# A four-layer hybrid of scans, convolutions and an FFT on one core: all stages rewritten with channels on partitions, norms by matrix products, and another packing of the scan

## The chip, the cores and the metric

The kernel runs on one core of one Trainium2 chip, in one launch. The metric is the device time in microseconds (us) of one execution. Everything is computed in fp32 except the two feed-forward blocks, which the reference quantizes (fp8 products, fp16 sums).

## The reference

The input `x` has 4 batches of 96 channels on a 64 x 64 grid, so 4096 positions a batch. Four layers follow each other:

```
# layer 0: state-space block in four directions, then a Gelu mlp
t = layernorm(x); xi, z = split(in_proj(t))            # 192 channels each
xi = silu(depthwise_conv3x3(xi))
for k in 4 directions:                                  # rows, columns, both reversed
    dts, Bs, Cs = x_proj[k](xi)                         # 6 + 16 + 16 rows
    dt = softplus(dt_proj[k](dts))                      # 192 channels
    h  = scan over 4096 positions:  h*exp(dt*A) + dt*B*x    # 192 channels x 16 states
    y += sum over states of h*C,  + D*x
t = x + out_proj(layernorm(y) * silu(z));  x = t + mlp(layernorm(t))   # 96 -> 384 -> 96
# layer 1: x + scan block in two directions with one state, conv 3x3, group norm before, layer norm + gate after
# layer 2: t + attention by FFT: relu(bn(x w1)), fft over 4096 positions, relu of a complex
#          scaling, inverse fft, w2, bn;   then t + quantized ffn(norm(t))
# layer 3: t + linear attention with 6 heads (q (k^T v)), then t + quantized ffn(norm(t))
```

The scan of layer 0 is the bulk: 4 batches x 4 directions x 192 channels x 16 states, each 4096 positions long.

## The kernel before

For each batch the stages run one after another: `l0_front`, `l0_scan`, `l0_tail`, `l1`, `l2_front`. Then one `l2_middle` handles the 64 middle frequencies of all four batches, and for each batch `l2_back`, `ffn`, `l3_attn`, `ffn` and `finish` end the work. A tile framework puts the waits; each engine takes its instructions in the order in which the code emits them. On SP the transfers are issued in that order too.

**Norms.** Layer norms reduce over channels, so `to_tokens` transposes 128 positions at a time through TensorE (L134), `normalize` makes the statistics with bn_stats (L148) and scales token by token on VectorE (L154), and `to_channels` transposes back (L162).

**Front.** The depthwise convolution is nine matmuls with diagonal weights (`dg`, made on GpSimd) for each block of 512 positions, accumulated in PSUM (L220). It runs for three groups of 64 channels, contracting 64 rows, and writes each result to 128 partitions, twice the same 64 channels: the scan wants them doubled.

**Scan.** Partitions are (2 states, 64 channels). A step takes 1024 positions of one direction; there are 4 directions x 4 steps a batch. The prelude of a step computes `px` (L266, with strided reads of `xi` in the column directions), copies it to `xd` on ScalarE (L271), sends B and C to DRAM, computes `dt` (L284 to L289) and `u` (L291). Then come 8 pairs of states x 3 channel groups = 24 iterations:

```
act(h, dts[d], AF.Exp, scale=negA[...])       # ScalarE, into PSUM (2 buffers)
nc.gpsimd.tensor_mul(w, us[d], bb)            # L310
nc.vector.tensor_tensor_scan(h, h, w, ...)    # L315 reversed, L319 forward
nc.scalar.copy(state, last column of h)       # L322, not in a direction's last step
nc.vector.tensor_mul(w, h, cc)                # L323
```

`bb` and `cc` are rows of B and C, spread over 64 partitions by DMA from DRAM. The sum over states is a matmul with a stacked identity (`idup`, L329 and L334) that accumulates in PSUM over the whole step; at the end of a step VectorE adds the sums to `y01` and `y2` (L337, L340).

**The rest.** `l0_tail` computes the gate z from the norm it kept in DRAM (`xn_d`), gates, projects and runs the mlp. `l1` works on whole rows of 4096 positions: its convolution is L465, its output projection L528. The FFT is split as 64 x 64: `l2_front` does the first half, `l2_middle` the twiddled second half and the inverse's first half, `l2_back` the inverse's second half (L656). `ffn` rounds to fp16 and fp8 on ScalarE and VectorE (L702 to L711).

Of the kernel before, what the change touches and what calls it, by code (L numbers as in the profile page):

```python
# [10 lines left out]
F32 = mybir.dt.float32  # L11
F16 = mybir.dt.float16
# [8 lines left out]
NB = L // 128  # L21
DI = 192
NS = 16
CH = 1024
NCH = L // CH
WBUFS = 6
POOL_OUT = 0
TABLES = {AF.Exp: "natural_log_exp_and_others", AF.Ln: "natural_log_exp_and_others"}
OTHER = (AF.Silu, AF.Gelu, AF.Sqrt)

_VECS = [
    ("g1", 1), ("b1", 1), ("bi01", 1), ("bi2", 1), ("bz01", 1), ("bz2", 1),
    ("cw01", 9), ("cw2", 9), ("cb", 3), ("dtb", 12), ("A", 96), ("D01", 4), ("D2", 4),
    ("og01", 1), ("ob01", 1), ("og2", 1), ("ob2", 1), ("opb", 1), ("g2", 1), ("b2", 1),
    ("mb1", 3), ("mb2", 1),
    ("l1cw", 9), ("l1cb", 1), ("l1dtb", 2), ("l1A", 2), ("l1D", 2), ("l1og", 1), ("l1ob", 1),
    ("l1sc", 1), ("f2b1", 3), ("f3b1", 3),
# [9 lines left out]
def tile_hybrid(ctx: ExitStack, tc: tile.TileContext, I: dict, out: bass.AP):  # L49
    nc = tc.nc  # L50
    n_evac = [0]

    def evac(o, i):
        n_evac[0] += 1
        if n_evac[0] % 2:
            nc.scalar.copy(o, i)
        else:
            nc.vector.tensor_copy(o, i)

    table = dict(now=None, load=None, users=[])  # L60
# [23 lines left out]
    const = ctx.enter_context(tc.tile_pool(name="const", bufs=1))  # L84
    dram = ctx.enter_context(tc.tile_pool(name="dram", bufs=1, space=DRAM))

    ident = const.tile([128, 128], F32, name="ident")
    make_identity(nc, ident)

    idup = const.tile([128, 2, 64], F32, name="idup")  # L90
    for h in range(2):
        s = slice(h * 64, h * 64 + 64)
        for j in range(2):
            nc.vector.tensor_copy(idup[s, j, :], ident[s, s])
    eps5 = const.tile([128, 1], F32, name="eps5")
    nc.vector.memset(eps5, 1e-5)
    one = const.tile([128, 1], F32, name="one")
    nc.vector.memset(one, 1.0)
    vec = const.tile([128, NVEC], F32, name="vec")
    nc.sync.dma_start(vec, I["vec"])  # L100

    def V(name, rows=128, j=0, n=1):
        c, w = _COL[name]
        assert j + n <= w
        return vec[0:rows, c + j : c + j + n]

    xn_d = dram.tile([B, C, L], F32, name="xn_d")
    t_d = dram.tile([B, 128, NB * C], F32, name="t_d")
    f1_d = dram.tile([64, 2, 64, B, DI], F32, name="f1_d")
    g1_d = dram.tile([B, 2, 64, 64, DI], F32, name="g1_d")  # L110


    negA = const.tile([128, 96], F32, name="negA")
    act(negA, V("A", n=96), AF.Exp)
    nc.vector.tensor_scalar_mul(negA, negA, -1.0)
    l1A = const.tile([128, 2], F32, name="l1A")
    act(l1A, V("l1A", n=2), AF.Exp)
    nc.vector.tensor_scalar_mul(l1A, l1A, -1.0)
    dsum = const.tile([128, 3], F32, name="dsum")
    nc.vector.reduce_sum(dsum[:, 0:1], V("D01", n=4), axis=mybir.AxisListType.X)  # L120
    nc.vector.reduce_sum(dsum[0:64, 1:2], V("D2", 64, n=4), axis=mybir.AxisListType.X)
    nc.vector.reduce_sum(dsum[0:C, 2:3], V("l1D", C, n=2), axis=mybir.AxisListType.X)


    def to_tokens(srcs, width, xt, ps):

        per = 4 if width == C else 2
        for g in range(NB // per):
            pt = ps.tile([128, 512], F32, tag="ps", name="pt_in")
            for j in range(per):  # L130
                blk = g * per + j
                off = j * width
                for ap, rows in srcs:
                    nc.tensor.transpose(  # L134
                        pt[:, off : off + rows], ap[:, blk * 128 : blk * 128 + 128], ident[:rows, :rows]
                    )
                    off += rows
            evac(
                xt[:, g * per : (g + 1) * per, :],
                pt[:, 0 : per * width].rearrange("p (j c) -> p j c", c=width),  # L140
            )

    def normalize(xt, xn, pool):
        stats = pool.tile([128, NB, 6], F32, tag="lnst", name="lnst")
        mv = pool.tile([128, NB, 2], F32, tag="lnmv", name="lnmv")
        rs = pool.tile([128, NB], F32, tag="lnrs", name="lnrs")
        for k in range(NB):
            nc.vector.bn_stats(stats[:, k, :], xt[:, k, :])  # L148
        for k in range(NB):
            nc.vector.bn_aggr(mv[:, k, :], stats[:, k, :])  # L150
        act(rs, mv[:, :, 1], AF.Sqrt, bias=eps5)
        nc.vector.reciprocal(rs, rs)
        for k in range(NB):
            nc.vector.tensor_scalar(  # L154
                xn[:, k, :], xt[:, k, :], mv[:, k, 0:1], rs[:, k : k + 1], ALU.subtract, ALU.mult
            )

    def to_channels(xn, g, off, rows, ps):

        pt = ps.tile([128, 512], F32, tag="ps", name="pt_out")  # L160
        for j in range(4):
            nc.tensor.transpose(pt[0:rows, j * 128 : j * 128 + 128], xn[:, 4 * g + j, off : off + rows], ident)  # L162
        return pt[0:rows, :]

# [7 lines left out]

    def psum(name, bufs):
        return dict(name=name, bufs=bufs, space=PSUM)

    def l0_front(b, xi):
        st, (wp, wk, ps) = pools(sb("l0f"), sb("l0f2", 2), psum("l0fp", 8))  # L180
        w_in = wp.tile([C, DI], F32, name="w_in")
        nc.sync.dma_start(w_in, I["w_inT"][:, 0:DI])
        x = wp.tile([C, L], F32, name="x")
        for q in range(4):
            nc.sync.dma_start(x[:, q * CH : (q + 1) * CH], I["x"][b, :, q * CH : (q + 1) * CH])
        xt = wp.tile([128, NB, C], F32, name="xt")
        to_tokens([(x, C)], C, xt, ps)
        normalize(xt, xt, wp)

        dg01 = wp.tile([128, 9, 128], F32, name="dg01")  # L190
        dg2 = wp.tile([64, 9, 128], F32, name="dg2")
        idf = idup.rearrange("p a b -> p (a b)")
        for t in range(9):
            nc.gpsimd.tensor_scalar(dg01[:, t, :], idf, V("cw01", 128, t), None, ALU.mult)  # L194
            nc.gpsimd.tensor_scalar(dg2[:, t, :], idf[0:64], V("cw2", 64, t), None, ALU.mult)
        xp01 = wp.tile([128, 66, 66], F32, name="xp01")
        xp2 = wp.tile([64, 66, 66], F32, name="xp2")
        nc.gpsimd.memset(xp01, 0.0)
        nc.gpsimd.memset(xp2, 0.0)
        for g in range(8):  # L200
            pt = to_channels(xt, g, 0, C, ps)
            xn = wk.tile([C, 512], F32, tag="xn", name="xn")
            act(xn, pt, AF.Identity, scale=V("g1", C), bias=V("b1", C))
            nc.sync.dma_start(xn_d[b, :, g * 512 : (g + 1) * 512], xn)
            for xp, m0, m, bias in ((xp01, 0, 128, V("bi01")), (xp2, 128, 64, V("bi2", 64))):
                pi = ps.tile([128, 512], F32, tag="ps", name="pi")
                nc.tensor.matmul(pi[0:m], lhsT=w_in[:, m0 : m0 + m], rhs=xn, start=True, stop=True)
                nc.vector.tensor_scalar(
                    xp[:, 1 + 8 * g : 9 + 8 * g, 1:65],
                    pi[0:m].rearrange("p (h w) -> p h w", w=64), bias, None, ALU.add,  # L210
                )

        for d in range(3):
            r0 = 64 if d == 1 else 0
            xp, dg = (xp2, dg2) if d == 2 else (xp01, dg01)
            for g in range(8):
                pc = ps.tile([128, 512], F32, tag="ps", name="pc")
                for t in range(9):
                    kh, kw = divmod(t, 3)
                    nc.tensor.matmul(  # L220
                        pc.rearrange("p (h w) -> p h w", w=64),
                        lhsT=dg[r0 : r0 + 64, t, :],
                        rhs=xp[r0 : r0 + 64, 8 * g + kh : 8 * g + kh + 8, kw : kw + 64],
                        start=(t == 0), stop=(t == 8),
                    )
                act(xi[d][:, g * 512 : (g + 1) * 512], pc, AF.Silu, bias=V("cb", 128, d))
        st.close()

    def l0_scan(b, xi, y01, y2):


        st, (ck, wk, ph, ps, dp) = pools(
            sb("l0c", 2), sb("l0w", WBUFS), psum("l0hp", 2), psum("l0sp", 1),
            dict(name="l0d", bufs=3, space=DRAM),
        )
# [5 lines left out]
        for k in range(4):  # L241
# [7 lines left out]
            def view(ap, lo, n):  # L249

                if not col:
                    return ap[:, lo : lo + n]
# [669 lines left out]
```

## Time and profile before

| | |
|---|---|
| median of 3 runs | 11,112.8 us (11,093.09 to 11,119.98) |
| profiled execution | 11,114.38 us, span 11,112.6 us |
| mean granted TensorE clock | 0.692 of full |
| VectorE (DVE) busy | 7171.7 us, 65% |
| TensorE (PE) busy | 8037.6 us, 72% |
| GpSimd (POOL) busy | 4701.3 us, 42% |
| ScalarE (ACT) busy | 3760.3 us, 34% |
| DMA | 713.27 MB, mean 64 GB/s |

The profile is one execution. Its slices cut the span into 40 equal parts, each digit the busy tenths of an engine; PEclk is the granted TensorE clock in tenths. A group row gives line, engine, operation, output and inputs, count, busy time, the mean duration in ns of one, and the idle time of the engine just before with what ended it. A row of windows gives, for a stretch of the span, its length, each engine's busy time, the granted clock, the share of the DMA engines and GB/s. Each fp32 matmul shows as two records. The batches follow each other about 2413 us apart; the middle of layer 2 begins at 9677 us and the four backs at 9993 us.

### The profile page before, as it was taken

What the parts mean: (1) busy time and instruction counts of PE and PEld (TensorE: products, weight loads), DVE (VectorE), ACT (ScalarE), POOL (GpSimd) and SP (SyncE); (2) the same over time, 40 slices, a digit from 0 to 9 for tenths busy, and PEclk for the clock granted to TensorE, in tenths of its full rate; (3) what the DMA queues carried; (4) which work ended last, traced back from release to release, by engine and by line L of the source; (5) the groups of instructions that cost most, each with busy time, mean ns of one, the idle gap of its engine ahead of it and who ended that gap; (6) DMA issues with size and microseconds to landing.
All of it is one profiled execution on the core that took longest, in us unless ns stands there. A gap on an engine that the chain in (4) does not pass through costs nothing. (4 is left out here: it accounts for less than half of the span.)

```text
span 11112.6 us, 64945 instructions
## 1 busy us (share of the span) xinstructions
PE 8037.6 (72%) x18840; PEld 2774.3 (25%) x18840; DVE 7171.7 (65%) x8167; ACT 3760.3 (34%) x5408; POOL 4701.3 (42%) x2174
## 2 busy tenths in 40 slices
PE   9776675869776766788766767697766768696666
PEld 3111111233111112233111112242111112244445
DVE  1688888340888887322888895415888883425555
ACT  1444443221444442213444442214444432211111
POOL 0677775000777772003777771005777750020000
PEclk9666666867667667757666667667666668695555
DMA  0233332010333331011333330012333330261110
GB/s 12 74 90 86 89 88 76 4 42 9 93 87 89 89 89 51 1 42 40 89 87 89 88 90 25 14 29 65 87 88 89 89 85 5 55 189 48 38 37 30
DMA packets 270938, 713.27 MB, mean 64 GB/s; under 512 B 49638, under 2 KB 106480, under 8 KB 269172
## 3 DMA queue, kind: packets, MB, share of 16 engines
q1 hardware_dynamic: 262388, 683.95, 23.1%
q0 software_dynamic: 8192, 25.17, 0.6%
q8 instruction: 149, 2.44, 0.1%
q14 instruction: 209, 1.71, 0.1%
HBM read 631.34 MB, written 77.59 MB: 64 GB/s over the span
## 5 line engine op out<-in xcount | busy, mean ns | idle before, releaser
L310 POOL TENSOR_TENSOR w<-u,bb 128x1024 f32<-128x1024 f32 x1536 | 3574.7, 2350 | 1323.7 <-PE py L329 1133.9
L329 PE MATMUL py<-w,idup 128*64 128x512 f32 x4096 | 2374.7, 965 | 1165.1 <-DVE w L323 1157.1
L75 ACT ACTIVATE h<-dt,negA 128x1024 f32<-128x1024 f32 x1536 | 1703.5, 1117 | 954.5 <-DVE w L323 947.3
L323 DVE TENSOR_TENSOR w<-h,cc 128x1024 f32<-128x1024 f32 x1536 | 1800.6, 1210 | 217.4 <-ACT state L322 217.4
L334 PE MATMUL py<-w,idup 128*64 128x512 f32 x2048 | 1144.1, 909 | 586.8 <-DVE w L323 586.8
L319 DVE TENSOR_TENSOR_SCAN h<-h,state,w 128x1024 f32<-128x1024 f32 x576 | 1324.3, 2345 | 97.8 <-ACT h L75 69.2
L315 DVE TENSOR_TENSOR_SCAN h<-h,state,w 128x1024 f32<-128x1024 f32 x576 | 1324.4, 2345 | 77.2 <-ACT h L75 50.0
L329 PEld LDWEIGHTS py<-w,idup 128*64 128x64 f32 x4096 | 524.3, 192 | 2858.7 <-DVE w L323 1796.7
L319 DVE TENSOR_TENSOR_SCAN h<-h,w 128x1024 f32<-128x1024 f32 x192 | 431.9, 2287 | 1211.9 <-POOL w L310 1152.6
L289 POOL TENSOR_TENSOR dt<-dt,rl 128x1024 f32<-128x1024 f32 x192 | 451.3, 2350 | 1796.5 <-DMA cc<-bc 790.4
L220 PE MATMUL pc<-xp,dg 64*128 64x512 f32 x1728 | 975.6, 750 | 0.0
L266 PE MATMUL px<-xi,xw 64*80 64x512 f32 x768 | 685.6, 1010 | 61.9 <-ACT state L322 29.5
L284 PE MATMUL pd<-xd,dtw 6*128 6x512 f32 x768 | 561.4, 818 | 183.9 <-ACT rl L67 142.9
L322 ACT COPY state<-h 128x1 f32<-128x1 f32 x1152 | 183.1, 159 | 1467.3 <-DVE h L315 768.7
L220 PEld LDWEIGHTS pc<-xp,dg 64*128 64x128 f32 x1728 | 403.6, 237 | 575.1 <-issue 574.0
L334 PEld LDWEIGHTS py<-w,idup 128*64 128x64 f32 x2048 | 250.6, 187 | 1186.5 <-DVE w L323 852.5
L291 POOL TENSOR_TENSOR u<-dt,xi 128x1024 f32<-128x1024 f32 x192 | 499.1, 2599 | 11.0
L67 ACT ACTIVATE dt<-pd,vec 128x512 f32<-128x512 f32 (+1 forms) x448 | 307.5, 686 | 531.8 <-PE pd L284 320.9
L315 DVE TENSOR_TENSOR_SCAN h<-h,w 128x1024 f32<-128x1024 f32 x192 | 430.0, 2285 | 44.5 <-ACT h L75 36.7
L194 POOL TENSOR_SCALAR dg<-idup,vec 128x128 f32<-128x128 f32 x36 | 21.4, 596 | 847.4 <-issue 847.0
L75 ACT ACTIVATE xi<-pc,vec 128x512 f32<-128x512 f32 x96 | 66.0, 687 | 893.2 <-PE pc L220 893.2
L621 POOL DMA_DIRECT2D g_d<-o x128 | 79.3, 624 | 603.4 <-DVE o L619 597.4
(210 smaller groups left out, 8339.2 us busy)
## 6 DMA issues: line engine op xcount, KB each, us to landing
bb<-bc SPq DMA_DIRECT2D x1024, 256.0 KB
cc<-bc SPq DMA_DIRECT2D x1024, 256.0 KB
f_d<-fo SPq DMA_DIRECT2D x64, 384.0 KB
a<-f_d SPq DMA_DIRECT2D x64, 384.0 KB
g_d<-o POOLq DMA_DIRECT2D x128, 192.0 KB, 4.0
gt<-g_d SPq DMA_DIRECT2D x32, 768.0 KB
bc<-xd SPq DMA_DIRECT2D x128, 64.0 KB
x<-in_x SPq DMA_DIRECT2D x16, 384.0 KB
```

Of the source, the lines that this page charges most:

```text
L75: r = nc.scalar.activation(o, i, func, **kw)
L220: nc.tensor.matmul(pc.rearrange("p (h w) -> p h w", w=64), lhsT=dg[r0 : r0 + 64, t, :], rhs=xp[r0 : r0 + 64, 8 * g + kh : 8 * g + kh + 8, ...
L266: nc.tensor.matmul(like(px[0:80]), lhsT=xw[:, d, :], rhs=view(xi[d][0:64], lo + hf * 512, 512), start=(d == 0), stop=(d == 2),)
L284: nc.tensor.matmul(pd, lhsT=dtw[:, d, :], rhs=xd[0:6, s], start=True, stop=True)
L289: nc.gpsimd.tensor_add(dt, dt, rl)
L291: nc.gpsimd.tensor_mul(like(u), like(dt), view(xi[d], lo, CH))
L310: nc.gpsimd.tensor_mul(w, us[d], bb)
L315: nc.vector.tensor_tensor_scan(o[:, ::-1], h[:, ::-1], w[:, ::-1], first, ALU.mult, ALU.add)
L319: nc.vector.tensor_tensor_scan(o, h, w, first, ALU.mult, ALU.add)
L323: (nc.gpsimd if pool_out else nc.vector).tensor_mul(w, o, cc)
L329: nc.tensor.matmul(py01[d * 64 : d * 64 + 64, s], lhsT=idup[:, 0, :], rhs=ws[d][:, s], **flags)
L334: nc.tensor.matmul(py2[hf * 64 : hf * 64 + 64], lhsT=idup[:, 0, :], rhs=ws[2][:, s], **flags)
```

## The change

The kernel is rewritten. Positions stay on the free axis and channels on partitions in all stages, so `to_tokens`, `normalize` and `to_channels` go. The main pieces:

- **Norm.** A matmul with the centring matrix `cent`, a Square on ScalarE, a matmul with `avg` for the variance, Ln and Exp(-0.5 x) on ScalarE, a multiply on VectorE.
- **Front.** Convolution of 128 channels at a time, then 64 channels x 2 halves of the grid. The gate z is computed here and kept in DRAM (`z_d`). `xi` goes to DRAM in row order and in column order (`xi_d`); GpSimd makes the transposed copy.
- **Scan.** Partitions are (32 channels, 4 states). Two times 3 groups of 32 channels x 4 quartets of states = 24 iterations a step as before, but `dt`, `u`, `bb` and `cc` are all spread by DMA from DRAM, the prelude works on [128, 3, 512] without doubling, the state copy is issued behind the C product, and the reduction is two matmuls of 32 columns an iteration with `sel4` that end after four iterations. The Y addition runs three times a step, into `Y` in SBUF. The prelude of the next step is emitted piece by piece between the iterations (`advance`). Y goes to DRAM at the end (`y_d`).
- **Tail, l1, FFT, back.** Each block of 512 positions goes through its whole chain before the next; `x1_d`, `t_d` and `t2_d` in DRAM hold the blocks between stages. `l2_middle` runs for each batch, so its tables `wf` and `wi` are loaded four times. The stages are generators; `drain` runs one to its end before the next begins (`OVERLAP` is False).

The core of the diff:

```diff
-    def to_tokens(srcs, width, xt, ps): ...
-    def normalize(xt, xn, pool): ...
-    def to_channels(xn, g, off, rows, ps): ...
+    def norm(x, o, wk, **kw):
+        pc = bank()
+        mm(pc[0:C], lhsT=cent, rhs=x, start=True, stop=True)
+        yield
+        sq = wt(wk, C, "sq")                      # (inside variance)
+        act(sq, pc[0:C], AF.Square)
+        pv = bank()
+        mm(pv[0:C], lhsT=avg, rhs=sq, start=True, stop=True)
+        yield
+        act(rs, pv[0:rows], AF.Ln, bias=eps5[0:rows])     # (inside rstd)
+        act(rs, rs, AF.Exp, scale=-0.5)
+        nc.vector.tensor_tensor(o, pc[0:C], rs, ALU.mult, **kw)
...
     # front, convolution
-        for d in range(3):
-            r0 = 64 if d == 1 else 0
-            xp, dg = (xp2, dg2) if d == 2 else (xp01, dg01)
-            for g in range(8):
-                for t in range(9):
-                        lhsT=dg[r0 : r0 + 64, t, :],
-                        rhs=xp[r0 : r0 + 64, 8 * g + kh : 8 * g + kh + 8, kw : kw + 64],
+        for part in range(2):
+            rows = 64 if part == 0 else 32
+            xp = (xp01, xp2)[part]
+            for g in range(0, rows // 8, 2):
+                for i in range(2):
+                    for t in range(9):
+                            lhsT=dg[:, t, :],
+                            rhs=xp[:, r : r + 8, kw : kw + 64],
...
     # scan, one iteration
-                        act(h, dts[d], AF.Exp, scale=negA[:, k * 24 + j : k * 24 + j + 1])
-                        nc.gpsimd.tensor_mul(w, us[d], bb)
-                            nc.vector.tensor_tensor_scan(o, h, w, first, ALU.mult, ALU.add)
-                            nc.scalar.copy(state[:, j : j + 1], o[:, last : last + 1])
-                        (nc.gpsimd if pool_out else nc.vector).tensor_mul(w, o, cc)
+                    act(h, dt, AF.Exp, scale=negA[:, k * 24 + n : k * 24 + n + 1])
+                    nc.gpsimd.tensor_mul(w, u, d["bb", q])
+                        nc.vector.tensor_tensor_scan(h, h, w, first, ALU.mult, ALU.add)
+                    nc.vector.tensor_mul(w, h, d["cc", q])
+                    if s < NCH - 1:
+                        nc.scalar.copy(state[:, n : n + 1], h[:, last : last + 1])
+                    for f in range(2):
+                        r = p * 64 + f * 32
+                        if col:
+                            o = py[r : r + 32].rearrange("p (w c h) -> p w c h", c=4, h=8)
+                            v = w.rearrange("p (w c f h) -> p f w c h", c=4, f=2, h=8)[:, f]
+                        else:
+                            o, v = py[r : r + 32], w[:, f * HC : (f + 1) * HC]
+                        mm(o, lhsT=sel4, rhs=v, start=(q == 0), stop=(q == 3))
+                    if n >= 3:
+                        advance(i + 1)
...
     # scan, prelude of a step
+            px = bank()
+            for j in range(3):
+                mm(px, lhsT=xw[:, j, :], rhs=xi[:, j, :], start=(j == 0), stop=(j == 2))
+            act(xd, px, AF.Identity, bias=V("ones"))
+            for j in range(3):
+                mm(pd, lhsT=dtw[:, j, :], rhs=xd[0:64], start=True, stop=True)
+                act(dtu[:, 0, j], pd, AF.Abs)
+                act(rl[:, j], pd, AF.Relu)
+            act(dtu[:, 0], dtu[:, 0], AF.Exp, scale=-1.0)
+            act(dtu[:, 0], dtu[:, 0], AF.Ln, bias=one)
+            nc.gpsimd.tensor_add(dtu[:, 0], dtu[:, 0], rl)
+            nc.gpsimd.tensor_mul(dtu[:, 1], dtu[:, 0], xi)
...
+        def load_du(i, m):                        # one group of four iterations ahead
+                nc.sync.dma_start(x, src.unsqueeze(1).to_broadcast([32, 4, CH]))
...
     # order of the stages
-    l2_middle()
+    for b in range(B):
+        n1 = drain(front(b), 8)
+        scan(b, sp, lambda: None)
+        n2 = drain(post(b), 8)                    # tail, l1, l2_front, l2_middle, back
```

In `back`, the first loop takes each block of 512 through projection, `ffn` of layer 2 (with its norm), the norm of layer 3 and the sum of k^T v; the second loop takes it through the attention's output and the `ffn` of layer 3 (with its norm).

## The prediction

> **What bounds the kernel now.** I read the page's busy totals and slices first, then the stage windows, then the groups of instructions.
>
> ```profile
> PE 8037.6 (72%) x18840; PEld 2774.3 (25%) x18840; DVE 7171.7 (65%) x8167; ACT 3760.3 (34%) x5408; POOL 4701.3 (42%) x2174
> PE   9776675869776766788766767697766768696666
> DVE  1688888340888887322888895415888883425555
> ```
>
> No engine bounds the whole. Four plateaus with DVE at 0.8 are the four scans; the valleys between them, and the last 1,100 us, belong to no engine. So each stage needs its own sum. The windows of batch 0, then the middle of all batches and the back of batch 0:
>
> ```profile
> core 0: us, PE busy (x) PEld busy (x) DVE busy (x) ACT busy (x) POOL busy (x), PEclk, DMA share, GB/s
> 63.00:310.00 247.00, 247.00 (x436) 101.04 (x436) 1.50 (x2) 24.28 (x26) 0.00 (x0) 1.00 0.00 1
> 337.00:1892.00 1555.00, 1062.20 (x1902) 245.32 (x1902) 1367.55 (x816) 691.46 (x983) 1126.22 (x479) 0.67 0.33 88
> 1990.00:2049.00 59.00, 50.71 (x128) 21.37 (x128) 13.54 (x41) 23.96 (x33) 0.00 (x0) 0.93 0.00 0
> 9677.00:9993.00 316.00, 304.02 (x768) 126.30 (x768) 61.31 (x64) 52.42 (x65) 78.36 (x127) 0.97 0.65 188
> 10057.00:10086.00 29.00, 25.53 (x120) 25.28 (x119) 7.31 (x26) 0.00 (x0) 0.00 (x0) 0.50 0.04 13
> 10086.00:10158.00 72.00, 34.04 (x180) 18.39 (x180) 61.22 (x255) 18.97 (x37) 0.00 (x0) 0.53 0.01 3
> ```
>
> The depthwise convolution (first row) is pure PE at full clock; the scan (second) has DVE busy 88%; where PE is busy half of a stage (last row) the granted clock is 0.53, where it is busy 0.86 to 0.96 it is 0.93 to 0.97, though the short matmuls of the row from 10057 stayed at 0.50 with PE busy 88%.
>
> ```profile
> L323 DVE TENSOR_TENSOR w<-h,cc 128x1024 f32<-128x1024 f32 x1536 | 1800.6, 1210 | 217.4 <-ACT state L322 217.4
> L319 DVE TENSOR_TENSOR_SCAN h<-h,state,w 128x1024 f32<-128x1024 f32 x576 | 1324.3, 2345 | 97.8 <-ACT h L75 69.2
> L310 POOL TENSOR_TENSOR w<-u,bb 128x1024 f32<-128x1024 f32 x1536 | 3574.7, 2350 | 1323.7 <-PE py L329 1133.9
> L75 ACT ACTIVATE h<-dt,negA 128x1024 f32<-128x1024 f32 x1536 | 1703.5, 1117 | 954.5 <-DVE w L323 947.3
> L220 PE MATMUL pc<-xp,dg 64*128 64x512 f32 x1728 | 975.6, 750 | 0.0
> L465 PE MATMUL pc<-xp,dg 96*96 96x512 f32 x576 | 247.9, 592 | 0.0
> L528 PE MATMUL po<-yn,w_out 96*96 96x512 f32 x64 | 64.5, 1111 | 72.4 <-DVE yn L526 44.8 <-issue 27.6
> ```
>
> One scan iteration costs DVE 2.35 + 1.21 us; POOL's 2.35 and ACT's 1.12 + 0.16 lie beside it. An fp32 matmul of 512 columns is two records; in the timeline records of a dense run start 0.429 us apart at full granted clock and 0.853 at half. A lone one (L528, half clock) takes 2.02 us from start to end, so 1.02 at full.
>
> Stages of before, in us: front with convolution 310 (300 for later batches), convolution end to scan end 1582, tail 157, l1 291, l2_front 89; the middle 316 for all, 79 a batch; back with both ffns, attention and finish 280. Together 2778 x 4 = 11,112, the profiled span (11,112.6; 11,114.4 with what lies around it). The median, 11,112.8, agrees, so I add nothing.
>
> **Convolution and front: -128 a batch.** Before issues 3 x 8 x 9 = 216 matmuls = 432 records; 144 of them (first third, rows 0 to 63) start 0.853 apart, 288 at 0.429: 123 + 124 = 247. After contracts 128 rows and issues 72 + 36 = 108: 216 x 0.429 = 93, plus 6 for the second part's diagonal weights and 3 of ramp. Why the first third ran at half I can't see. The nearest row is the 96-row convolution, L465, all at 0.429; if the new one were all at 0.853 it would cost 92 more. Its front is four double blocks, each two norm chains (below), three projection groups and Silus, 15.5 to 16.5 us, plus 5 of start: 70, against 53 to 63. Sum 172 against 300.
>
> **Scan: -98.** Before works two scans, then two products: pairs take 6.97 us with state in the timeline, 3.485 an iteration, with steps 95.8 apart: 24 x 3.485 = 83.6 plus 12.2. Of these 12.2, some 6 are the end of a step (last product, PE reduction 3.85 us, y adds 1.2 to 2.4 and twice 0.7 to 1.25), some 6 are stalls; one is DVE standing 2.7 and 4.1 us while ACT, in its order, waits for px behind strided PE reads. After: scan and product alternate and each product waits for its own scan; such a pair costs 0.035 us more and loses the 0.085 overlap of independent successors, so 3.52 with state and 3.46 without (first of four steps): 24 iterations 84.1. The state copy behind the product no longer delays it (L323's 217.4 us of idle are 0.14 an iteration, mostly inside the pair I measured). Three Y additions of about 0.9 (L340 shape, now 128 x 512) sit between a scan and its product, so PE's reduction is covered: 2.7. Prelude stalls: ACT still takes px and pd in order, and behind a waiting xd, Abs or Relu stand the next state copy and the exp h that DVE needs two iterations on; ACT has 2.15 us free in each 3.5. I take 2.5 a step, bounds 0 to 7. With 0.5 for column-order steps: 90, bounds 87 to 94. Start: the cold prelude (xi load, px, bc to DRAM, dt, dd to DRAM, broadcast) 40; end: writing 3.1 MB of Y and reading the first quarter back, 20 at the 188 GB/s of the window above. 16 x 90 + 40 = 1480 against 1582, and 20 that I book with the tail. DMA rises from 8 to about 12 MB a step, 134 GB/s: below the shown 188, so I cost it at nothing; if that cover fails, dt and u, issued on SP one group of four iterations ahead and behind dd's writes, come late six times a step.
>
> Reduction matmuls read w in runs of 8 elements in column-order steps. The row: L266's column-order steps, runs of one element 256 B apart, show at least 1.03 us a record, row-order ones 0.59; two records in two column tiles run side by side, so even at 1.03 an iteration's four records cost PE 2.1 us, under 3.5. The Trainium skill (SBUF — State Buffer, section Door 1: The DMA port swizzle, note on cachelines) has fp32 runs of four or more elements read at full rate; by it this term is zero. I take 0.5 a step, above.
>
> **Norm by TensorE.** One block of 512: lone matmul 2.07 (with hop), Square 0.66, lone matmul 2.07, Ln 0.72, Exp 0.66, multiply 0.73 = 6.9 us at half clock, 4.9 at full. Before normalised tokens densely: transposes at 0.35 to 0.40 a record, DVE at 0.24 and 0.33 a block. Stages drain one after another, so PE's own order lets no block overtake the last.
>
> **Tail: +73, plus 20.** Per 1024 columns 20 (means, variance, gating); per 512: projection 5.4 + 0.8, norm 6.9, first mlp matmuls and Gelu 6.1, second 5.4 = 24.6 at half clock: 4 x 20 + 8 x 24.6 = 277. At full the same chain gives 181. PE would be busy about three quarters of it, where the rows grant 0.71, so I take 230 against 157; bounds 181 and 277. Table loads (1283 ns each, two a block as Gelu and Ln alternate) I cost at nothing behind the matmuls; without that cover they are 20 a batch.
>
> The rule that speaks against this change is in the Trainium skill (TensorE: Matmul & The Clock Gate, HAM oscillation): PE returns to half rate after idle windows of about 3.4 us, and only sustained work lifts it. By it alone, the new gaps being below 3.4 us, the tail could warm up and hold at 181, while any longer gap would send it to 277. The rows show both, 0.53 for the ffn's alternation of PE and DVE and 0.93 for the dense mlp, and the new tail's three quarters lie between.
>
> **l1: -27.** Statistics 4, in-projection 14, convolution 65, weights 6, first direction 8 x 4.6 = 37, second with norm and gate 8 x 17.2 = 138 (20.3 at half): 264 against 291, to 289.
>
> **l2_front: 0.** Eight norms and reloads, 55 less overlap, replace transposes; the 89 stays, bounds 80 to 105.
>
> **Middle: +31.** Per batch now: 32 halves of two lone-ish matmul groups with a Relu and a copy between, 3.25 each, + 6 = 110 against 79; bounds 85 and 150. wf and wi are loaded four times: 21 MB a batch, at 188 GB/s 111 us, the same.
>
> **Back: +130.** 16 inverse blocks 62; 8 x 27.7 (projection, ffn, two norms, kv) = 222; 8 x 15 (projection, ffn, norm) = 120; 6 of small work; blocks reloaded from DRAM come a buffer ahead, at nothing: 410 against 280; bounds 380 and 440. The ffn rows (DVE 61 of 72 us) fall, but the chain through PE, ACT and DVE replaces throughput by latency.
>
> Sum a batch: -128 - 98 + 20 + 73 - 27 + 31 + 130 = +1. With 10 once for loads that is 11,127. I move to 11,180: each serial chain has more hand-offs than I priced, at 0.035 to 0.06 us each, some 14 us a batch.
>
> **Rivals.** First, faster: the alternating scan runs at its DVE sum, 87 a step, and dense projections hold the clock up: 16 x 3 = -48, tail 200 (-30), back 390 (-20), middle 100 (-10): -108 x 4, about 10,750. For it: DVE's 0.88, the 0.93 of the mlp window. Against: the 0.53 of the ffn window. Second, slower: serial chains keep the half clock and latency decides: tail 277 (+47), l1 289 (+25), middle 149 (+39), back 440 (+30): +141 x 4, about 11,740. It decides once the mean clock in those stages stays below about 0.6. For it: every stage with PE busy below 0.55 was granted 0.5. Third, the convolution stays at 0.853: +92 x 4 = 11,550; against it L465. Fourth, the change of layout doesn't shorten the step, because prelude stalls or late dt and u broadcasts keep 95 us: +80 x 4 = 11,500.
>
> **How the numbers follow.** About 0.3% (33 us) is what a measurement of this kernel can tell from no change. Forecast (within 250 of 11,180) 0.45, first rival 0.23, second 0.14, third 0.07, fourth 0.11. Below 11,080 lie the first rival and 0.16 of the forecast: 0.39; within 33 us 0.05; above, 0.56. The range takes the first rival's centre, most of rivals three and four, and stops short of the second: 10,720 to 11,680.
>
> **What would show it.** Right: all convolution records 0.43 apart; steps of about 90 us with DVE over 95% busy between their ends; the tail, middle and back longer than before with PE busy 50 to 75% at a clock of 0.5 to 0.75. Wrong: steps of 95 or more (stalls of ACT behind px or pd, or DMA-released waits of POOL and ACT); a front of over 200; a back below 330, which would mean that blocks overlap despite PE's order.

## The result and the profile after

The changed kernel takes 11,386.2 us (median of 4 runs, 11,385.1 to 11,393.2) against 11,103.7 us for the kernel before (4 runs): the ratio is 1.0254, interval 1.0237 to 1.0272, so it is 2.5% slower. The profiled execution took 11,387.0 us, its span 11,385.2, beside 11,114.4 before: +272.6. The forecast was 11,180 us, +0.6%. The side was right, the time lies in the range, and the loss is about four times the forecast one.

The page's totals and slices of the changed kernel:

```profile
PE 7041.0 (62%) x15736; PEld 2157.7 (19%) x15736; DVE 6363.4 (56%) x4750; ACT 3768.4 (33%) x5595; POOL 4240.9 (37%) x1840
PE   6555547675755554768565555476757555547675
DVE  1999981302199998220219999812021999981302
PEclk8565658755766565865575656686557565658655
```

Every engine but ScalarE has less busy time, PE by 1000 us and DVE by 800, and the kernel is slower: the time stands between the instructions. The plateaus of DVE (the scans) are now at 0.9; the valleys between them are longer. The granted clock fell from 0.692 to 0.637. The windows of batch 1 (stretch, length, busy time and count of PE, PEld, DVE, ACT and POOL, granted clock, share of the DMA engines, GB/s) are the front's norms, its convolution, the scan from its first to its last instruction, the tail, the middle and the back:

```profile
2845.00:2946.00 101.00, 80.10 (x116) 21.96 (x116) 7.04 (x13) 41.17 (x58) 0.00 (x0) 0.50 0.18 55
2946.00:3057.00 111.00, 98.14 (x216) 42.21 (x215) 0.00 (x0) 7.56 (x11) 11.71 (x11) 0.92 0.19 61
3102.00:4519.00 1417.00, 750.44 (x1712) 113.53 (x1712) 1358.10 (x815) 561.81 (x805) 1005.62 (x414) 0.61 0.45 142
4539.00:4735.00 196.00, 136.54 (x226) 46.71 (x226) 47.25 (x63) 63.45 (x76) 2.54 (x1) 0.79 0.13 38
5105.00:5292.00 187.00, 154.23 (x322) 88.94 (x320) 0.10 (x1) 32.35 (x68) 3.30 (x1) 0.51 0.42 117
5292.00:5686.00 394.00, 247.20 (x626) 116.19 (x627) 78.61 (x147) 97.85 (x185) 1.16 (x9) 0.55 0.11 33
```

With l1 (4735 to 5006) and l2_front (5006 to 5105) the stages of this batch stand against the forecast as follows, in us a batch:

| part | before | forecast | measured | off by |
|---|---|---|---|---|
| front and convolution | 300 | 172 | 212 | +40 |
| scan, from the convolution's end | 1582 | 1480 | 1462 | -18 |
| Y to DRAM and back | 0 | 20 | 20 | 0 |
| tail | 157 | 230 | 196 | -34 |
| l1 | 291 | 264 | 271 | +7 |
| l2_front | 89 | 89 | 99 | +10 |
| middle | 79 | 110 | 187 | +77 |
| back | 280 | 410 | 394 | -16 |

The misses sum to +66 a batch, +264 in all. The forecast had added 53 us for hand-offs, 10 for loads and, by a slip, 16 (its sum takes the scan as -98, where 1480 against 1582 is -102). Four batches like this one fall 22 us short of the measured time. Together 264 - 79 + 22 = 207, against a whole miss of 206. That the time lies in the range is partly luck: terms priced 68 us a batch too dear offset half of the 134 priced too cheap. The largest miss is the middle: it lost 108 us a batch against the kernel before, more than the bound of 150 allowed. One half of a quartet in the timeline of the middle (start, duration, engine, line; in brackets the idle time before, and what ended it):

```profile
5149.09 1.64 PE L745 MATMUL bg<-rib,sel 2*128 2x384 f32 x2
5150.66 1.65 PE L748 MATMUL bg<-a,wf 128*128 128x192 f32 x4
5152.41 0.49 ACT L58 ACTIVATE g<-bg 128x384 f32<-128x384 f32 x1 [2.73 <-PE bg L748]
5152.95 1.65 PE L755 MATMUL bg<-g,wi 128*128 128x192 f32 x4 [0.64 <-ACT g L58]
5154.53 1.64 PE L745 MATMUL bg<-rib,sel 2*128 2x384 f32 x2
```

From one L745 to the next are 5.44 us; 32 of them make 174. PE works in three bursts of 1.65 us and stands 0.64 us for the Relu. It is busy 82% of the window, yet granted 0.51.

The costliest groups of the scan, and the convolution:

```profile
L412 DVE TENSOR_TENSOR w<-h,cc 128x1024 f32<-128x1024 f32 x1536 | 1830.4, 1214 | 32.3 <-DVE h L411 0.5
L409 DVE TENSOR_TENSOR_SCAN h<-h,state,w 128x1024 f32<-128x1024 f32 x576 | 1333.2, 2346 | 36.6 <-ACT state L415 27.0
L253 PE MATMUL bg<-xp,dg 128*128 128x512 f32 x864 | 390.7, 615 | 75.9 <-DMA dg<-in_dg 75.9
```

The C product stood 217.4 us behind the state copy before and stands 32.3 us now; PE waited 75.9 us in all for the convolution's diagonal weights.

### The profile page after: what moved, and what is told of

Read it like the earlier page. It is cut to its first block, busy times and chain, and to the rows that moved or that the text cites. A ratio compares the mean times of both kernels' runs of the same rounds, so it can differ in the third digit from the quotient of the medians.

```text
span 11385.2 us, 55086 instructions
## 1 busy us (share of the span) xinstructions
PE 7041.0 (62%) x15736; PEld 2157.7 (19%) x15736; DVE 6363.4 (56%) x4750; ACT 3768.4 (33%) x5595; POOL 4240.9 (37%) x1840
## 4 chain that ended last, share of the span: by engine, by line
DVE 34%; PE 33%; issue 13%; ACT 12%; DMA 5%; POOL 2%; SPq 1%; DVEq 0%; ACTq 0%; POOLq 0%
DVE h L409 12%; DVE h L411 11%; DVE w L412 6%; ACT h L66 5%; PE bg L158 4%; PE bg L253 3%; PE bg L163 3%; ACT rs L66 2%; PE bg L567 2%; PE bg L755 2%; PE bg L748 2%; PE bg L745 2%; PE bg L496 1%; PE py L423 1%; ACT sq L58 1%
## 5 line engine op out<-in xcount | busy, mean ns | idle before, releaser
L423 PE MATMUL py<-w,sel 128*32 128x512 f32 x6144 | 2621.9, 984 | 2806.1 <-DVE w L412 2722.2
L412 DVE TENSOR_TENSOR w<-h,cc 128x1024 f32<-128x1024 f32 x1536 | 1830.4, 1214 | 32.3 <-DVE h L411 0.5
L423 PEld LDWEIGHTS py<-w,sel 128*32 128x32 f32 x6144 | 313.8, 136 | 5048.2 <-DVE w L412 4153.5
L158 PE MATMUL bg<-sq,avg 96*96 96x512 f32 x448 | 405.2, 1003 | 153.1 <-ACT sq L58 153.1
L253 PE MATMUL bg<-xp,dg 128*128 128x512 f32 x864 | 390.7, 615 | 75.9 <-DMA dg<-in_dg 75.9
L618 POOL TENSOR_TENSOR dt<-dt,u 96x512 f32<-96x512 f32 x64 | 83.2, 1300 | 938.2 <-ACT a L66 938.2
L58 ACT ACTIVATE sq<-bg 96x512 f32<-96x512 f32 x224 | 132.9, 593 | 823.4 <-PE bg L163 738.9
L269 POOL COPY xt<-xi 128x512 f32<-128x512 f32 x48 | 51.0, 1063 | 816.9 <-ACT xi L66 816.9
L66 ACT ACTIVATE rs<-bg,eps 96x512 f32<-96x512 f32 (+1 forms) x240 | 164.0, 683 | 476.3 <-PE bg L158 396.9
L755 PE MATMUL bg<-g,wi 128*128 128x192 f32 x512 | 210.8, 567 | 82.8 <-ACT g L58 82.8
L567 PE MATMUL bg<-xp,dg 96*96 96x512 f32 x576 | 247.9, 592 | 0.0
```

The source lines that it names most:

```text
L58: return nc.scalar.activation(o, i, func, **kw)
L66: r = nc.scalar.activation(o, i, func, **kw)
L158: mm(pv[0:C], lhsT=avg, rhs=sq, start=True, stop=True)
L253: mm(pc.rearrange("p (h w) -> p h w", w=WW), lhsT=dg[:, t, :], rhs=xp[:, r : r + 8, kw : kw + 64], start=(t == 0), stop=(t == 8),)
L412: nc.vector.tensor_mul(w, h, d["cc", q])
L423: mm(o, lhsT=sel4, rhs=v, start=(q == 0), stop=(q == 3))
```

## The experiments

**1. Three theories of the middle.** Is it the clock, the length of the chain, or the four-fold load of the tables? Three kernels, each from the changed one. The first only adds work:

```diff
                 act(g, px[:, 0 : 2 * DI], AF.Relu)
+                pq = bank()
+                mm(pq, lhsT=cover[:, 0:128], rhs=cover, start=True, stop=True)
```

> The changed kernel, with one more 512-column fp32 matmul of zeros into an unused bank in each of the middle's 32 halves a batch, placed while PE waits for the Relu. Clock theory (the middle took 188 us a batch, 5.44 us a half, because its matmul bursts never lift PE from the half clock, granted 0.51): the extra work lifts the clock to 0.9 or more, a half takes about 3.5 us, the middle 115 to 130 us a batch, the kernel about 11,130 us. Latency theory (the chain PE, ACT, PE, ACT alone, whatever the clock): a half grows by about 1.1 us, the middle to 222, the kernel to about 11,520. Table theory (the four-fold loads of wf and wi bind): no change, 11,386, or a little more.

Measured: 11,120.8 us (10 runs; 1.0013 of the kernel before, 1.0004 to 1.0023), 265 us less than the changed kernel, with 128 matmuls more. The window of one middle, and its timeline:

```profile
5052.00:5172.00 120.00, 111.14 (x387) 62.78 (x385) 0.46 (x3) 32.76 (x69) 1.77 (x1) 0.93 0.60 183
```

```profile
5101.95 0.91 PE L747 MATMUL bg<-rib,sel 2*128 2x384 f32 x2
5102.79 0.92 PE L750 MATMUL bg<-a,wf 128*128 128x192 f32 x4
5103.55 1.02 PE L755 MATMUL bg<-cover 128*128 128x512 f32 x2
5104.40 0.86 PE L760 MATMUL bg<-g,wi 128*128 128x192 f32 x4
5105.20 0.91 PE L747 MATMUL bg<-rib,sel 2*128 2x384 f32 x2
```

PE is now busy 93% and granted 0.93, every burst is nearly halved, and a half takes 3.25 us with one burst more in it; that burst lies within the wait for the Relu. The second kernel reorders:

```diff
                 act(g, px[:, 0 : 2 * DI], AF.Relu)
-                py = bank()
-                ... (second matmuls of this half)
+                if todo is not None:
+                    second(*todo)       # second matmuls of the half before
+                todo = (kq, h, g, wi, o)
```

> The changed kernel with the middle pipelined by one half: the first matmuls of the next half are issued ahead of the second matmuls of this one, so PE doesn't wait for the Relu. Clock theory: PE gets dense, the clock rises to 0.9 or more, a half takes 2.6 to 3.5 us (the lower end would meet the transfers, 22 MB a batch at the 188 GB/s of the kernel before, 117 us), the middle 110 to 120 us a batch, the kernel about 11,100. Latency theory with the clock left at half: 1.64 + 1.65 + 1.65 us a half, 165 a batch, the kernel about 11,290. Table theory: no change.

Measured: 11,101.3 us (10 runs; 0.9995 of the kernel before, 0.9986 to 1.0004). Its middle:

```profile
5020.00:5133.00 113.00, 97.06 (x321) 65.22 (x320) 0.00 (x0) 31.19 (x65) 1.63 (x1) 0.79 0.69 193
```

113 us at 193 GB/s, beside 188 in the kernel before: here the transfers come within reach of setting the time. PE waits 9.9 us for its input blocks and is granted 0.79. The third loads the tables of the first quartet and uses them for all sixteen, so it leaves out the other fifteen loads:

```diff
-            wf = wk.tile([128, 4, 128], F32, tag="wf", name="wf")
-            nc.sync.dma_start(wf, I["c_wf"][kq])
+            if kq == 0:
+                wf = wp.tile([128, 4, 128], F32, name="wf")
+                nc.sync.dma_start(wf, I["c_wf"][kq])
     (wi likewise)
```

> The changed kernel with the twiddle tables wf and wi of the first quartet loaded once a batch and used for all sixteen; the reload of the other fifteen is left out, 7.9 of 22 MB a batch. Clock and latency theories: nothing waits for these loads, the middle stays at 185 to 188 us a batch, the kernel within 15 us of 11,386. Table theory: the middle falls in proportion to the bytes, to about 120 a batch, the kernel to about 11,110.

Measured: 11,381.2 us (4 runs; 1.0248, 1.0233 to 1.0263), its middle 184 us with PE granted 0.51 at 76 GB/s. The bytes fell by a third and the time by 3 us. So the middle's loss is the half clock: PE doesn't get out of it while it stands 0.64 us in every 5.44, and it does once a dense burst fills the gap. L745, a third of PE's time, contracts only 2 rows; that alone doesn't hold PE at half, since the kernel before runs much the same mix without such gaps (PE busy 96%) at 0.97. Whether the gap alone would was not tried.

**2. The back: chains that wait.** Blocks in pairs, emitted alternately:

```diff
-        for g in range(NG):
+        def block1(g):
             ...
+        yield from paired(block1, range(NG), 2)     # next piece of one, then of the other
```

> The changed kernel with the blocks of both loops of the back taken two at a time, their pieces emitted alternately, and two buffers for h1, hq and skv. Latency theory (one block is a chain of PE, ACT and DVE steps of 27.4 us in the first loop and 15 in the second, and no engine is full): two chains share that time, a pair of blocks takes 33 to 38 us instead of 55, and 18 to 20 instead of 30; the back falls from 399 to about 285 us a batch, the kernel to about 10,930. Rival (the back is bound by an engine or by transfers, PE at half clock above all): less than 100 us in all, above 11,290.

Measured: 10,823.3 us (4 runs; 0.9743, 0.9719 to 0.9768), 563 us less than the changed kernel, with the same instructions. The back:

```profile
5160.00:5412.00 252.00, 196.68 (x620) 106.22 (x621) 71.65 (x138) 93.42 (x183) 1.76 (x9) 0.66 0.18 51
```

394 us became 252; PE, busy 63% in the changed kernel, is busy 78%, and the clock rises from 0.55 to 0.66 besides. The expected 285 had no term for the clock: PE's busy time for these records fell by 50 us. With this one repair the kernel is 280 us under the kernel before.

**3. The convolution's weights.** Both `dg` tiles loaded at the front's start:

```diff
+        for i in range(2):
+            nc.sync.dma_start(dgs[i], I[("dg01", "dg2")[i]])
         (before the norms; in each part: dg = dgs[part])
```

> The changed kernel with both sets of diagonal convolution weights loaded at the front's start instead of at each part's start. If the waits in the trace (6.3 and 12.9 us a batch, released by the load of dg) are on the path: -19 x 4 = -77, about 11,310. If the loads then delay x and w_in at the front's start: half of that or nothing. Nothing else of the front moves: its norms stay at the half clock, 85 us a batch.

Measured: 11,282.8 us (4 runs; 1.0152, 1.0126 to 1.0179): -103, where the waits alone were 76. Part of the rest, some 7 us a batch, is the half clock that a part starts with. In the changed kernel the first 4 to 7 records of each part start 0.85 us apart or more. With early weights the second part follows the first without a gap, and its records are 0.43 apart from the start: from the first record to the last the convolution of batch 1 takes 94.3 us instead of 110.9, 12.9 of it the wait and some 3.7 the clock. Where the last 3 us a batch went is not shown.

**4. The state copy.** Its place, undone in the changed kernel:

```diff
+                    if s < NCH - 1:
+                        nc.scalar.copy(state[:, n : n + 1], h[:, last : last + 1])
                     nc.vector.tensor_mul(w, h, d["cc", q])
-                    if s < NCH - 1: ...
```

> The changed kernel with the state copy issued ahead of the C product again, as in the kernel before. If the wait for the copy (0.16 us and two hand-offs, about 0.2 us) stands in the DVE's path each time: 1152 x 0.2 = 230 us, the kernel about 11,610. If DVE's order puts another scan between, as in the kernel before, the wait is covered and the alternating pair's 0.085 us of lost overlap comes back: between 11,300 and 11,400.

Measured: 11,393.9 us (4 runs; 1.0258, 1.0241 to 1.0275), no difference from 1.0254. And done alone in the kernel before:

```diff
-                        if step < NCH - 1:
-                            nc.scalar.copy(state[:, j : j + 1], o[:, last : last + 1])
                         (nc.gpsimd if pool_out else nc.vector).tensor_mul(w, o, cc)
+                        if step < NCH - 1: ...
```

> The kernel before with the one part alone: the state copy issued behind the C product. Theory: the copy's place is worth nothing, as it was in the changed kernel, since another scan lies between on DVE: within 30 us of 11,101. Rival: the 217 us that DVE stands before the C product, released by the state copy, go: 10,890 to 11,050.

Measured: 10,962.9 us (4 runs; 0.9871, 0.9856 to 0.9886), -143: the rival holds, and this one part of the change alone makes the kernel before 1.3% faster. The C product's group in this kernel:

```profile
L320 DVE TENSOR_TENSOR w<-h,cc 128x1024 f32<-128x1024 f32 x1536 | 1851.5, 1219 | 85.4 <-DVE h L319 0.9 <-issue 0.9 <-PE pd L284 0.5
```

Its wait for the copy, 217.4 us before, is gone. The copy itself takes 0.16 us, and the pairs in the steady part of a step show no wait for it. It stood behind what ScalarE had in front of it, here in the kernel before:

```profile
583.55 0.58 ACT L271 COPY xd<-px 80x512 f32<-80x512 f32 x1 [6.68 <-PE px L266]
584.03 0.16 ACT L322 COPY state<-h 128x1 f32<-128x1 f32 x1
584.22 1.23 DVE L323 TENSOR_TENSOR w<-h,cc 128x1024 f32<-128x1024 f32 x1 [4.18 <-ACT state L322]
```

ScalarE waits for px, copies it to `xd`, and only then takes the state copy that DVE waits for. In the trace 215.6 of the 217.4 us stand at a state copy right behind such an `xd` copy. The wait is not all saved: the scans now wait 162 us for state copies, 21 before, while their waits for the exponential h fell from 188 to 72 us. Over half of the iterations now alternate (scan, product, scan, product), at 3.59 us instead of 3.485, so part of the gain was given back. In the changed kernel the same order costs nothing; there the `xd` copy waits little for px, 19 us in the scan of one batch (state_first) beside 149 in the kernel before.

**5. The convolution's slow third.** The forecast left open why the first 144 of 432 records a batch run at half rate. Its windows were of batch 0, where the granted clock reads 1.00 from the span's start to the first change on record. In batch 1 of the kernel before the same stretches read:

```profile
2485.00:2606.00 121.00, 121.00 (x144) 47.64 (x145) 0.74 (x1) 4.81 (x7) 0.00 (x0) 0.50 0.00 0
2606.00:2729.00 123.00, 123.00 (x291) 53.79 (x288) 0.00 (x0) 18.40 (x18) 0.00 (x0) 0.98 0.00 0
```

So it is the clock: PE busy 100% for 121 us and granted half. Two orders of the three groups in the kernel before:

```diff
-        for d in range(3):
+        for d in (1, 0, 2):          # b_conv
+        for d in (0, 2, 1):          # b_conv2
```

> The kernel before with its three convolution groups in the order 1, 0, 2 (rows 64 to 127 of xp01 first, then rows 0 to 63, then xp2). In before the first 144 of 432 records a batch start 0.853 us apart, the others 0.429. If the slow third belongs to its place (it comes first, after sparse matmuls), it stays first, now with rows 64 to 127, and the time stays within 20 us of 11,101. If it belongs to rows 0 to 63 of that tile, it moves to second place, same time. If neither, all records are 0.429 apart: -62 us a batch, 10,850.

Measured: 11,112.3 us (10 runs; 0.9996, 0.9981 to 1.0012). The slow records are the first 144 again, now those of rows 64 to 127. The rows themselves are not slow.

> The kernel before with its convolution groups in the order 0, 2, 1: the first two groups now both read rows 0 to 63, and the step to rows 64 to 127 comes at the second boundary instead of the first. In batches 1 to 3 of the kernel before PE is busy 100% of the first group with 64-row matmuls, granted 0.50 for its 121 us, and 1.00 within 3 us of the second group's start. Theory (a dense run of 64-row matmuls doesn't lift the clock, and what lifts it is the boundary, where matmuls of the other 64 rows overlap the last of this group): the half clock lasts for two groups, 288 records 0.85 apart, +61 us a batch, about 11,350. Rival (the boundary itself, a new tile, or some 120 us of work lift it, whatever the rows): 144 slow records as before, within 20 us of 11,105.

Measured: 11,347.5 us (4 runs; 1.0216, 1.0199 to 1.0233), 240 us more for an exchange of two groups. In batch 1 the first group begins at 2541 us; the second and the third follow:

```profile
2664.00:2787.00 123.00, 123.00 (x150) 48.63 (x149) 0.00 (x0) 9.20 (x9) 0.00 (x0) 0.50 0.00 0
2787.00:2847.00 60.00, 60.00 (x142) 25.81 (x139) 0.00 (x0) 9.20 (x9) 0.00 (x0) 1.00 0.00 0
```

In the trace 288 records a batch start 0.85 us apart, and the third group's 0.43: the half clock lasts through some 243 us of unbroken 64-row matmuls, until the run steps to the other 64 rows. Neither 243 us of time, nor a new tile, nor the boundary lifts it; that step does. Once lifted, a run of 64-row matmuls keeps the clock: in the kernel before the second and third groups run at 0.98, the third on rows 0 to 63 again. That overlapping matmuls of the two row groups are what lifts it fits, but was not tried by itself. The 128-row convolution of the changed kernel lifts the clock within 8 records. Of the 136 us a batch that the convolution gained (247 to 111), 61 are the clock; the rest is half the records, less the waits for the weights.

**6. The repairs together, and the stages under the scan.** First the pipelined middle, early weights and pairs in the front's norms, the tail, l1 and the back:

> The middle pipelined by one half, dg early, and blocks taken two at a time in the front's norms, the tail, l1's two loops and the back. If the losses of the changed kernel are serial chains at the half clock, the parts add: middle -285, dg -77, back -460, tail 196 to 130 a batch (-260), l1 loops 175 to 125 (-200), front 85 to 60 (-100): about 10,000 us, under both kernels. If pairs only move the wait to PE at half clock or to ACT: about 10,600.

Measured: 9,935.6 us (4 runs; 0.8949, 0.8918 to 0.8980). Windows of batch 1 (front with convolution, tail, back):

```profile
2464.00:2646.00 182.00, 163.49 (x340) 62.44 (x339) 12.69 (x24) 52.51 (x78) 11.71 (x11) 0.81 0.20 63
4113.00:4282.00 169.00, 119.93 (x225) 43.29 (x224) 47.26 (x63) 51.92 (x68) 1.62 (x1) 0.82 0.21 65
4709.00:4960.00 251.00, 196.11 (x620) 103.42 (x621) 71.77 (x138) 93.17 (x181) 2.01 (x9) 0.67 0.20 55
```

Then the changed kernel with the post stages of one batch and the front of the next emitted between the scan's iterations:

```diff
-        scan(b, sp, lambda: None)
-        n2 = drain(post(b), 8)
+        side = chain(post(b - 1), front(b + 1))
+        scan(b, sp, tick)               # tick: about two pieces of side an iteration
```

> The changed kernel with the post stages of one batch and the front of the next emitted between the iterations of the scan that runs between them (one or two pieces an iteration), with one PSUM bank for the prelude and two for the stages, single buffers in l1's loops and in the back, and the three Gelu and gate products taken one bank at a time. Only the first front and the last post stand alone. If DVE sets the time there (96% busy in the scan; the hidden stages add 240 to 260 us a batch): 211 + 4 x 1460 + 3 x 260 + 1170 = 8,000 us. If ACT's order or PE at half clock (750 us of the scan plus some 900 of the stages) sets it: 4 x 1460 grows by 500 a batch, 8,800. If the stages' waits at the heads of the queues stop the scan for their whole latency: no gain, about 11,000.

Measured: 9,636.7 us (4 runs; 0.8674, 0.8652 to 0.8696), between the expected cases: in batch 1 a step with hidden stages takes 90 to 186 us instead of 88, and one 283. In that one stands this window:

```profile
3394.00:3558.00 164.00, 86.31 (x135) 22.60 (x133) 37.17 (x61) 39.07 (x64) 5.96 (x11) 0.54 0.12 36
```

GpSimd does 6 us of work in 164; one scan starts at 3394.6, the next at 3558.8. The last kernel puts a pause between the post stages and the next front, and takes the pipelined middle and, where stages stand alone, the pairs:

```diff
+            work.append(iter(range(40)))       # pieces without work
             work.append(front(b + 1))
```

> The overlap kernel with the pipelined middle, blocks in pairs in the first front and the last post, and a pause of some 20 iterations between the last piece of a batch's post stages and the next front. In overlap DVE stood 164 us in one step of two batches: GpSimd's memset of the next front's padding waited for the back to free that memory, and the products w stood behind it. If that is the cause: -150 x 2, the last post 1170 to 830, together about 9,000. If the hole has another cause: 9,300.

Measured: 8,880.8 us (4 runs; 0.7994, 0.7980 to 0.8007), a fifth under the kernel before. In batch 1 the 283 us step is 108, but steps of 195 and 168 us follow where the front now starts, with no scan for 82 us once: this step and the next three take 577 us instead of 642. So the pause recovers at most 65 of the 164. The trace of overlap shows that the memset was not the whole cause: it waited 92.6 us and started at 3502.3, but GpSimd then stood another 63.4 us before its next product, and ScalarE issued no exponential h from 3391.5 to 3557.6, only pieces of the stages. Why so many of these stood together in its order is not shown. The rest of the gain is the end of the kernel after the last scan (1,229 us to 855) and the steps with post stages under them, 117 us in each of two batches, with the pipelined middle among them. The scan of batch 1 with its hidden stages:

```profile
1690.00:3940.00 2250.00, 1585.26 (x4022) 467.05 (x4020) 1679.40 (x1212) 971.90 (x1452) 1092.39 (x471) 0.77 0.43 133
```

## Why the prediction was right and wrong

**Right: the scan.** Alternating iterations start 3.53 us apart with state and 3.46 without (forecast 3.52 and 3.46); steps average 88.6 us (90 forecast, bounds 87 to 94). But only 680 of the 1,536 iterations alternate; the others still go two by two, as 1,528 do in the kernel before. Both kernels emit scan and product in turn, so DVE's order is not simply the order of the code. As pairs cost 3.485 an iteration, the price held either way. POOL and the transfers stayed covered at 142 GB/s. The step came out 1.4 us shorter than priced.

**Right: the convolution's records**, 0.43 us apart but for the first 4 to 7 of each part, and the chains: a block of the back's first loop starts 27.4 us after the last (27.7 forecast). That these chains set the back, and not an engine, is shown by the pairs.

**Wrong: the middle, the step that failed.** It said "32 halves ... 3.25 each". 3.25 us is what a half costs near the full clock: the cover kernel, at 0.93, shows exactly that. At the clock that the changed kernel was granted, 0.51, a half costs 5.44: the term measured 187 us where 110 was forecast, 308 us over four batches, more than the whole miss. The upper bound of 150 was no bound either, since three bursts of 1.65 us alone make 158. Two things hid it: the transfer estimate gave 111, "the same", and two prices that agree look like a confirmation; and the clock was weighed in the tail and the second rival, but not put into this term. The row that should have warned was in the prediction itself: PE busy 88% of a window of short matmuls and granted 0.50.

**The clock.** The Trainium skill (TensorE: Matmul & The Clock Gate, sections Part 1 and HAM oscillation) has some 3.4 us of sustained work lift PE to full rate, and names idle gaps above that as what sends it back. Here the middle stayed at 0.51 for 187 us though PE's gaps, but for two at its start, were 0.9 us or less, and the convolution of b_conv2 stayed at half rate through 243 us without a gap. The measurements decide: gaps far shorter than 3.4 us can keep a stage at half, and a run without any gap can stay there too. In the convolution it counts which rows the matmuls occupy: 64 rows don't lift the clock, 128 do. In the middle the gap counts, filled by a burst of 128 rows or by the next half. That the two cases have one cause is not shown.

**Wrong by less: the front (+40).** The four double blocks took 84 us where 62 to 66 were priced, in batch 0 as in batch 1 (72 us each from the first norm to the last), since they run at the half clock; x came after a wait of 6.5 us at the start; and the diagonal weights cost 19 us of waits, where 6 were priced. The step "pure PE at full clock", of the kernel before, misread batch 0's 1.00. Front and convolution together came to 212; "a front of over 200" was one of the forecast's own signs of being wrong.

**Too dear: the tail (-34).** It was granted 0.79 and came near its full-clock end (181). So the second rival's mechanism was real, but in other stages than its price assumed: it held in the middle, the front and the back (0.50 to 0.55), not in the tail and l1 (0.79 and about 0.77).

**The state copy** had no price in the forecast: its wait was called "mostly inside the pair I measured". The pairs had no such wait; it sat in 80 stalls, 60 of them of 2.7 to 5.2 us. The forecast described such stalls ("2.7 and 4.1 us") but didn't connect them with the copy, and put them down to "strided PE reads": 112 of the 217 us fall in the row directions, which have no strided reads.

## What to carry to other kernels

Price a chain that PE shares with another engine at the half clock as well as the full one, in every stage. Here a stage at the half clock was repaired by giving PE work in the gap: in the middle matmuls of zeros showed the cause (187 us to 120) and the next half's own matmuls did as well (113), in the back the next block's own work did it (394 to 252). Two estimates that agree confirm each other only if they can't both be wrong in the same direction: look for the assumption (here the clock) that only one of them has. And try the parts of a rewrite alone: here the move of one statement in the old kernel gave 143 us, while the rewrite that contained it lost 280.

## What the runs showed of the hardware

A dense run of 64-row fp32 matmuls that starts at the half clock stays there, 0.50 granted at 100% busy, for as long as it lasts here: 121 us in the kernel before, 243 us when two such groups follow each other. The step to the other 64 rows ends it, and 64-row matmuls after it run at 0.98. The same convolution with 128 rows is at full rate within 8 records. PE busy 82% in bursts, a third of them of 2 rows, was granted 0.51 through a whole stage; with one 128-row burst more in each gap it was granted 0.93, and the stage took 120 us instead of 187. Much the same bursts without such gaps, PE busy 96%, were granted 0.97 in the kernel before. And the clock that the profile shows before its first change is no measurement: in batch 0 it reads 1.00 where the records' spacing shows half.
